# A graph-attention kernel on one core: the next block's preparation spread unevenly over the groups, and further ahead

## The chip, the cores and the metric

The kernel runs on one core of a Trainium2 chip. Its time is device microseconds of one execution. Five engines work side by side, each through its own instructions in the order in which the program issued them: TensorE (PE; matrix products and transposes into PSUM), VectorE (DVE), ScalarE (ACT), GpSimd (POOL; here almost only the issue of gathers by index) and SyncE (SP; the issue of plain transfers). An engine that meets an instruction whose inputs are not there waits, and what stands behind it on that engine waits too.

## The reference

3327 rows (padded to 3328) of 128 features, and a sparse adjacency matrix `adj` with some 64 non-zeros in a row. Layer 0 is an attention with four heads, layer 1 a normalised neighbourhood sum:

```python
    h = jnp.maximum(_layernorm(x, axis=-1), 0.0)
    for each head:
        x1 = h @ w1;  x2 = h @ w2
        E = leaky_relu(x1[:, None, :] + x2[None, :, :], 0.01)
        s = exp(tanh((E @ a) / 8.0) * 8.0) * adj
        s = s / sum(s, axis=-1)
        out = leaky_relu(s @ h @ Wlin.T, 0.01)
    x = x + concatenate(heads) @ w
    # layer 1
    h = jnp.maximum(_layernorm(x, axis=-1), 0.0)
    A = adj + I;  D_inv = A.sum(1) ** -0.5
    x = x + relu((D_inv[:, None] * A * D_inv[None, :]) @ (h @ W.T + b))
```

The scores are wanted only where `adj` is not zero.

## The kernel before

**Blocks, halves, groups.** The rows are cut into 26 blocks of 128. For each row the kernel finds the columns of its non-zeros, gathers those columns' projections from a table in memory (`g`, L597, by GpSimd, 64 gathers a block, plus 4 into `ge`), and works on what it gathered. A block has two halves of 64 rows, a half has nine groups (`NG`, L252). Groups 0 to 7 of a half take two per gathered unit `w`, with 512 pairs of row and column for each head. The ninth group (`m == 8`) takes the overflow buffer `ge`: rows with more neighbours than their slots hold. Counted through a block the groups are 0 to 17; the ninth ones are 8 and 17.

**A group.** `stage_z` (L612) transposes the gathered projections on PE into PSUM `z` (L624), in two parts of two heads with two buffers between them; DVE takes the maximum with the negated projection of the row (L640, 128x1024 values for each part) into `r`. In the ninth group z is made of 8 transposes, four small ones (L627) and four products (L629), DVE's maximum covers only 64 columns a head (L635), and ACT takes the rest with a relu (L637). `stage_r` (L645) then makes the scores with products `s` (L653); it is issued one group behind. After every second group, `finish` (L657) copies the scores (ACT), turns them (PE, L671), adds and weighs them (DVE, L674 to L693, or L709 and L711 for the overflow), and sums with the products `ag` (L702, L721). At the end of a half `close` (L727) finishes the rows.

**The preparation.** `prep(b)` (L353) is a generator that readies block b in at most 72 steps (`NPREP`), each ended by a `yield`. In this order: it makes codes of the non-zeros of a quarter of the columns at a time (DVE, L410), looks through them with eight-wide maxima (L422), and between those turns the block of `adj` (PE, four transposes L365; ACT copy L367; a store to `AT_d`, L370) and multiplies the turned pieces with rows of layer 1 that are already known (`known_step`, PE L379, DVE L385). How many are known grows with the block (`finished`, L345): none up to block 3, up to 22 columns of blocks in the last. Then it takes sums (ACT, L443), asks for the next block of `adj` (L351), selects the lists of columns (DVE, L453 and L456), makes the indices (L463 to L473), handles the overflow (L489 to L546), and projects the block's own rows (PE, `x1b` L553 and `x1n` L559).

**What sets the order.** Nothing reorders the instructions afterwards: the order on each engine is that of the calls. The main loop (L1195) goes over all 468 groups and calls `slot()` six times for each: once before `stage_z`, four times in it, once behind `stage_r`. `slot` (L858) counts places, lets the pending `finish` and `close` generators take a step, and advances the preparation to a step that follows from the count; then it issues gathers for which buffers are free:

```python
        SLOTP = 6 * 2 * NG                       # 108 places a block
        t = state["slot"] / SLOTP
        advance(NPREP * (1 + t + min(1.0, t) * AHEAD))
```

So a block's 72 steps of preparation go evenly over 108 places, two thirds of a step to a place, four steps to a group. With `AHEAD = 0.5`, at the start of block b the preparation of block b+1 stands at its step 36, and that of block b+2 begins with group 9.

Of the kernel before, what the change touches and what calls it, by code (L numbers as in the profile page):

```python
# [231 lines left out]
def _sparse_layers(tc, nc, x, adj, w1, w2, a, wlin, w, gw, gb, gb_sb, gwT, x_sb, dinv, flag, ident, out):  # L232
# [19 lines left out]
    NG = 9  # L252
# [4 lines left out]
    with ExitStack() as l0:  # L257
# [87 lines left out]
        def finished(b):  # L345

            return max(0, 4 * (b // 4) - 2)
# [262 lines left out]


        def stage_z(k, hb, m, slot):  # L612
            n = 4 * P if m < 8 else FOUND * P
            arrived(k, hb, m // 2)
# [30 lines left out]
        def stage_r(k, hb, m, rs):  # L645
            n = 4 * P if m < 8 else FOUND * P + HALF
            at = m % 2
            if state["scores"] is None:
                state["scores"] = ps_s.tile([P, BANK], F32, name="s")
                nc.vector.memset(state["scores"], 0.0)  # L650
            k.s = state["scores"]
            for h in range(H):
                nc.tensor.matmul(k.s[32 * h:32 * h + 2, :n], sel[:, h, 31 - at:33 - at], rs[h // 2][:, h % 2, :n],  # L653
                                 start=(at == 0), stop=(at == 1 or m == 8))
# [151 lines left out]
        NLIST = 42  # L806
        NPREP = 72
        SLOTP = 6 * 2 * NG
        AHEAD = 0.5
        preps = [prep(b, blks[b]) for b in range(NB)]  # L810
        queue = deque()
        done = [0] * NB
        state = {"slot": 0, "fetched": 0, "g": 4, "ge": 1}
        state["early"], state["turn"], state["scores"] = None, -1, None
        ends, tails = [], []

        def advance(upto):

            for b in range(NB):
                while done[b] < NPREP and b * NPREP + done[b] < upto:  # L820
                    if next(preps[b], "end") == "end":
                        done[b] = NPREP
                    else:
                        done[b] += 1
                        assert done[b] < NPREP

        def fetch():
            while state["fetched"] < len(fetches):
                b, hb, w = fetches[state["fetched"]]
                kind = "ge" if b < NB and w == NW else "g"  # L830
                if state[kind] == 0 or (b < NB and not blks[b].ready):
                    return
                state[kind] -= 1
                if b == NB:
                    strip(pieces[w])
                else:
                    gather(b, hb, w)
                    if w == LATE and hb == (b == 0) and b + 1 < NB:
                        queue.append((None, 0, 0, partial(weights, b + 1)))
                state["fetched"] += 1  # L840
# [4 lines left out]
        def issue():  # L845

            queue.popleft()[-1]()

        def trickle():
            while queue:  # L850
                issue()
# [4 lines left out]
                issue()  # L856

        def slot():  # L858
            state["slot"] += 1
            t = state["slot"] / SLOTP  # L860
            for todo in (tails, ends):
                todo[:] = [f for f in todo if next(f, "end") != "end"]
            advance(NPREP * (1 + t + min(1.0, t) * AHEAD))
            fetch()
            trickle()
            if state["early"] is not None and next(state["early"], "end") == "end":
                state["early"] = None
# [6 lines left out]
        early = {s: range(finished(4 * s), finished(4 * s) + BEGUN) for s in (1, 2, 3) if finished(4 * s) + BEGUN < NB - 3}  # L874
# [24 lines left out]
        def begin():  # L899

            work = [(s, j) for s in early for j in early[s]]
            pairs = [work[i:i + PAIR] for i in range(0, len(work), PAIR)]
            if not work:
                return
            thirds = pa.tile([P, NP], F32, name="adjb")[:, :3 * PAIR * BANK].rearrange("p (k j i) -> p k j i", k=3, j=PAIR)

            def bring(k):
                if k < len(pairs):
                    for to, of in columns(thirds[:, k % 3], pairs[k]):
                        nc.sync.dma_start(to, of)  # L910

            for k in range(3):
                bring(k)
            for _ in range(14):
                yield
            po = None
            for i, (s, j) in enumerate(work):
                assert blks[j].closed
                if j == early[s][0]:
                    po = bank()  # L920
                nc.tensor.matmul(po, x_sb[:, j, :], thirds[:, i // PAIR % 3, i % PAIR], start=(j == early[s][0]), stop=(j == early[s][-1]))
                if i % PAIR == PAIR - 1:
                    bring(i // PAIR + 3)
                if j == early[s][-1]:
                    part2 = pv.tile([P, H, P], F32, name="outT").rearrange("p h i -> p (h i)")
                    nc.scalar.copy(part2, po)
                    nc.sync.dma_start(part2_d[:, 4 * s * P:4 * s * P + BANK], part2)
                for _ in range(4):
                    yield
# [44 lines left out]
        def layer1():  # L974
            ending, sums, ins = [], {}, {}
            for i, (s, j) in enumerate(work):
                if i == in_front:
                    yield "all"
                w = min(4, NB - 4 * s) * P
                if s not in sums:  # L980
                    sums[s] = ps_z.tile([P, 2, BANK], F32, name="z")[:, 0]
                if j == min(NB - 1, first_column(s) + 4 * (s not in front)):
                    assert len(ending) < 2
                    ins[s] = strip_in(s)
                nc.tensor.matmul(sums[s][:, :w], x_sb[:, j, :], strips[s, j][:, :w], start=(j == first_column(s)), stop=(j == NB - 1))  # L985
                if i % PIECE == PIECE - 1 or i == len(work) - 1:
                    allow("g")
                ending[:] = [f for f in ending if next(f, "end") != "end"]
                if j == NB - 1:
                    ending.append(strip_out(s, sums.pop(s), *ins.pop(s)))  # L990
                yield "one"
            for e in ending:
                for _ in e:
                    pass

        groups = [(b, hb, m) for b in range(NB) for hb in range(2) for m in range(NG)]
# [192 lines left out]
        with tc.manual_schedule():  # L1189
            fetch()  # L1190
            while queue:
                issue()
            rs = {}
            n = len(groups)
            for i in range(-1, n + 1):  # L1195
                if i + 1 < n:
                    slot()
                if 0 <= i < n:
                    b, hb, m = groups[i]
                    if (b, hb, m) == (max(0, NB - 2), 1, 0):  # L1200
                        state["early"] = begin()
                    rs[i] = stage_z(blks[b], hb, m, slot)
                if 0 <= i - 1 < n:
                    b, hb, m = groups[i - 1]
                    stage_r(blks[b], hb, m, rs.pop(i - 1))
                    if m % 2 or m == NG - 1:
                        ends.append(finish(blks[b], hb, m // 2))
                    slot()
            lay = layer1()
            todo = "one"  # L1210
            while ends or tails or state["early"] is not None:
                slot()
                if todo == "one":
                    todo = next(lay)
            for _ in lay:
                fetch()
                assert not queue
# [60 lines left out]
def kernel(  # L1278
# [26 lines left out]
    gb_sb = const.tile([P, D], F32, name="gb_sb")  # L1305

    _sparse_layers(tc, nc, x, adj, w1, w2, a, wlin, w, gw, gb, gb_sb, gwT, x_sb, dinv, flag, ident, out)


# [46 lines left out]
```

## Time and profile before

| | us |
|---|---|
| median of 3 runs (lowest, highest) | 2523.51 (2521.55, 2527.58) |
| the profiled execution | 2520.29 |
| its span, from the first to the last instruction | 2518.6 |
| its mean granted TensorE clock | 0.982 |
| PE, DVE, ACT, POOL busy | 2283.0, 2091.0, 686.3, 1733.9 |
| first r of group 0 of block 0; of block 25 | 90.7; 2324.5 |

How the page is read. Busy time is the time in which an engine executes; matrix products are pipelined and their ends modelled, so a busy PE is not one at its peak. PEld is PE's loading of weights, which overlaps its products. The costliest groups name line, engine, operation, output<-inputs and the shape, then `xcount | busy us, mean ns | idle time of the engine just before them, and what ended most of it`. The waits name who waited for whom, in total, how often, and the longest. The starts of DVE's maxima (L640, L635) mark the groups in time: the two of each group stand in order, so the first one of every eighteenth group begins a block. Blocks 1 to 24 take 87.4 to 91.6 us each by these starts.

### The profile page before, as it was taken

How to read it: one execution, taken by the hardware profiler on the slowest of the kernel's cores; microseconds unless marked ns; L12 is line 12 of the kernel's file. 1: busy time of each engine (PE TensorE's matmuls, PEld its weight loads, DVE VectorE, ACT ScalarE, POOL GpSimd, SP SyncE). 2: the span in 40 equal slices, each digit the busy share in tenths (PEclk: the TensorE clock that was granted, in tenths of full speed). 3: DMA queues.
4: the chain of work that ended last, by engine and by line, in shares of the span. 5: the costliest groups of instructions: out<-in, count | busy, mean ns of one | idle time of the engine just before them, and what ended most of it. 6: DMA issues, size and time to landing. Idle time of an engine off the chain costs nothing.

```text
span 2518.6 us, 52430 instructions
## 1 busy us (share of the span) xinstructions
PE 2283.0 (91%) x19410; PEld 1577.3 (63%) x19410; DVE 2091.0 (83%) x6478; ACT 686.3 (27%) x1703; POOL 1733.9 (69%) x1822
## 2 busy tenths in 40 slices
PE   6589999989999898999999999999999999999987
PEld 4456666666666666666666666666666666666643
DVE  7688988898898889889889888988988898895623
ACT  4122223223223222322322232232222223222110
POOL 3577777777777776777777777777777777777700
PEclk9799999999999999999999999999999999999999
DMA  9999999999999999999999999999999999999995
GB/s 307 377 359 325 344 340 312 339 358 319 323 356 334 316 341 336 298 333 357 331 317 349 347 311 333 354 321 319 344 339 316 338 348 310 328 325 351 347 275 153
DMA packets 417844, 826.94 MB, mean 328 GB/s; under 512 B 38435, under 2 KB 288815, under 8 KB 414255
## 3 DMA queue, kind: packets, MB, share of 16 engines
q0 software_dynamic: 141440, 619.41, 70.2%
q1 hardware_dynamic: 165343, 147.87, 18.5%
q10 hardware_dynamic: 110800, 56.25, 7.7%
q8 instruction: 156, 2.56, 0.4%
q14 instruction: 105, 0.86, 0.1%
HBM read 754.47 MB, written 113.22 MB: 345 GB/s over the span
## 4 chain that ended last, share of the span: by engine, by line
PE 36%; DVE 27%; DMA 19%; POOL 10%; issue 7%; ACT 1%; SPq 0%; DVEq 0%; ACTq 0%; POOLq 0%
DVE r L640 13%; DMA g<-table,idx 11%; PE z L624 11%; POOL g L597 9%; PE s L653 6%; PE z L629 3%; DVE cand L422 3%; DMA AT_d<-at 3%; PE tr L671 2%; PE ag L702 2%; DVE cand L456 2%; DVE lists L453 2%; DMA g<-AT_d 2%; DVE codes L410 2%; PE z L985 1%
## 5 line engine op out<-in xcount | busy, mean ns | idle before, releaser
L597 POOL DMA_INDIRECT g<-table,idx x1664 | 1611.9, 969 | 606.1 <-issue 416.3
L640 DVE TENSOR_TENSOR r<-z,x1n 128x1024 f32<-128x1024 f32 x832 | 1009.9, 1216 | 33.2 <-PE z L624 31.4
L624 PE MATMUL z<-ident,g 128*128 128x128 f32 x6656 | 918.6, 279 | 127.5 <-DVE r L640 110.6
L624 PEld LDWEIGHTS z<-ident,g 128*128 128x128 f32 x6656 | 746.4, 142 | 334.7 <-DVE r L640 222.2
L653 PE MATMUL s<-r,sel 128*2 128x512 f32 (+1 forms) x3744 | 473.6, 578 | 2.6 <-DVE s L650 1.9
L662 ACT COPY ssb<-s 128x512 f32<-128x512 f32 x260 | 146.9, 565 | 470.9 <-PE s L653 462.5
L422 DVE MAX8 cand<-codes 128x8 f32<-128x52 uint16 x1664 | 215.1, 204 | 0.0
L682 ACT ACTIVATE th<-sc 128x32 f32<-128x32 f32 x260 | 58.2, 224 | 459.8 <-DVE sc L677 422.3
L702 PEld LDWEIGHTS ag<-g,wt 128*32 128x32 f32 x3328 | 98.7, 110 | 120.3 <-issue 105.2
L671 PE MATMUL tr<-ident,ssb 128*128 128x128 f32 x988 | 157.0, 279 | 10.4 <-ACT ssb L662 9.0
L367 ACT COPY at<-tr 128x512 f32<-128x512 f32 (+1 forms) x175 | 97.1, 555 | 225.3 <-PE tr L365 194.1
L629 PE MATMUL z<-oi,x1b 128*128 128x256 f32 x416 | 145.4, 431 | 0.0
L453 DVE MAX8 lists<-cand 128x8 f32<-128x272 f32 (+1 forms) x338 | 133.2, 394 | 2.9
L702 PE MATMUL ag<-g,wt 128*32 128x133 f32 x3328 | 133.5, 278 | 1.5 <-DVE wt L693 1.5
L365 PE MATMUL tr<-ident,adjb 128*128 128x128 f32 x676 | 110.1, 287 | 25.2 <-DMA adjb<-in_adj_dram 17.7
L674 DVE TENSOR_TENSOR sc<-tr,g 128x32 f32<-128x32 f32 x208 | 38.5, 185 | 112.4 <-PE tr L671 112.4
L671 PEld LDWEIGHTS tr<-ident,ssb 128*128 128x128 f32 x988 | 111.0, 141 | 31.2 <-ACT ssb L662 23.4
L597 POOL DMA_INDIRECT ge<-table,idxo x104 | 98.8, 950 | 31.7 <-issue 14.0
L635 DVE TENSOR_TENSOR r<-z,x1n 128x128 f32<-128x128 f32 x104 | 29.9, 289 | 109.2 <-PE z L629 108.7
L637 ACT ACTIVATE r<-z 128x512 f32<-128x512 f32 x104 | 62.0, 597 | 212.5 <-DVE r L635 212.5
L456 DVE MATCH_REPLACE8 cand<-lists,cand 128x272 f32<-128x272 f32 (+1 forms) x312 | 118.1, 379 | 0.0
L410 DVE SCALAR_TENSOR_TENSOR codes<-adjb,code 128x832 uint16<-128x832 f32 x104 | 103.1, 1018 | 13.1 <-DMA adjb<-in_adj_dram 13.1
(201 smaller groups left out, 2446.0 us busy)
## 6 DMA issues: line engine op xcount, KB each, us to landing
adjb<-in_adj_dram SPq DMA_DIRECT2D x26, 1664.0 KB
table<-AT_d SPq DMA_DIRECT2D x26, 1664.0 KB
AT_d<-at ACTq DMA_DIRECT2D x150, 256.0 KB
g<-table,idx POOLq DMA_INDIRECT x1664
table<-img SPq DMA_DIRECT2D x12, 1296.0 KB
adjb<-AT_d SPq DMA_DIRECT2D x72, 128.0 KB
g<-AT_d SPq DMA_DIRECT2D x25, 256.0 KB
g<-AT_d ACTq DMA_DIRECT2D x25, 256.0 KB
```

Of the source, the lines that this page charges most:

```text
L410: nc.vector.scalar_tensor_tensor(codes[:, i], adjb[:, c0:c0 + part], 0.0, code[:, c0:c0 + part], op0=OP.not_equal, op1=OP.mult, accum_out= ...
L422: nc.vector.max(cand[:, c, 8:].rearrange("p (r s) -> p r s", s=32)[:, :, sgm % 32], codes.rearrange("p a b -> p (a b)")[:, sgm % 32 * SEG: ...
L453: nc.vector.max(top, of)
L456: nc.vector.match_replace(out=of, in_to_replace=top, in_values=of, imm_value=0.0)
L597: return nc.gpsimd.indirect_dma_start(out=g[:, t, lo:hi], out_offset=None, in_=tab, in_offset=bass.IndirectOffsetOnAxis(ap=at[:, t:t + 1], ...
L624: nc.tensor.matmul(z[:, i, q * P:(q + 1) * P], g[:, m % 2 * 4 + q, c0:c0 + D], ident, is_transpose=True, start=(q == 0 or m < 8), stop=(m ...
L629: nc.tensor.matmul(z[:, i, :n], k.x1b[:, h * D:(h + 1) * D], k.oi[:, hb * n:(hb + 1) * n], start=False, stop=True, skip_group_check=True)
L640: nc.vector.tensor_tensor(r.rearrange("p h (i s) -> p h i s", s=16), z.rearrange("p h (i s) -> p h i s", s=16), k.x1n[:, 2 * hp:2 * hp + 2 ...
L653: nc.tensor.matmul(k.s[32 * h:32 * h + 2, :n], sel[:, h, 31 - at:33 - at], rs[h // 2][:, h % 2, :n], start=(at == 0), stop=(at == 1 or m = ...
L662: nc.scalar.copy(ssb[:, :nk * P], s[:, :nk * P])
L671: nc.tensor.transpose(pt[:, q, :], ssb[:, q * P:(q + 1) * P], ident)
L702: nc.tensor.matmul(ag[32 * cg:32 * cg + 32, u, :WORK], wt[:, t].rearrange("p h q -> p (h q)"), g[:, t, f0:f0 + WORK], start=(w == 0 and t ...
```

## The change

Each place now counts with a weight. Before the places of a group are called, `state["pace"]` is set: 2.2 in the ninth groups, and (9 - 2.2) / 8 = 0.85 in the eight others of the half, so that a block still counts 108. The share of a block by which preparation runs ahead goes from 0.5 to 0.58, reached in the course of block 0.

```diff
-        AHEAD = 0.5
+        NINTH = 2.2
+        AHEAD = 0.58
...
-        state["early"], state["turn"], state["scores"] = None, -1, None
+        state["early"], state["turn"], state["scores"], state["pace"] = None, -1, None, 1
...
         def slot():
-            state["slot"] += 1
+            state["slot"] += state["pace"]
             t = state["slot"] / SLOTP
...
             for i in range(-1, n + 1):
+                if 0 <= i < n:
+                    state["pace"] = NINTH if groups[i][2] == NG - 1 else (NG - NINTH) / (NG - 1)
                 if i + 1 < n:
                     slot()
                 if 0 <= i < n:
```

In steps of preparation: 8.8 go into a ninth group and 3.4 into each other one, where all had 4. At the start of block b the preparation of block b+1 stands at step 41.8 of 72. Its last three steps and the first six of block b+2's fall into group 8 (the codes of the first half of the columns among them); the transposes and known products of block b+2 begin with group 9 in place of group 10; the last selections and the first list of indices fall into group 17.

## The prediction

> **What bounds the kernel now.** I read the page's busy shares and costliest groups first, then the waits by engine, then the busy time of each engine in stretches of two blocks, and last the program order of both builds against these durations.
>
> The page's busy line (busy us, share of the span, count), its chain shares, and four of its groups (busy, mean ns | idle before, releaser):
>
> ```profile
> PE 2283.0 (91%) x19410; PEld 1577.3 (63%) x19410; DVE 2091.0 (83%) x6478; ACT 686.3 (27%) x1703; POOL 1733.9 (69%) x1822
> PE 36%; DVE 27%; DMA 19%; POOL 10%; issue 7%; ACT 1%; SPq 0%; DVEq 0%; ACTq 0%; POOLq 0%
> L597 POOL DMA_INDIRECT g<-table,idx x1664 | 1611.9, 969 | 606.1 <-issue 416.3
> L640 DVE TENSOR_TENSOR r<-z,x1n 128x1024 f32<-128x1024 f32 x832 | 1009.9, 1216 | 33.2 <-PE z L624 31.4
> L635 DVE TENSOR_TENSOR r<-z,x1n 128x128 f32<-128x128 f32 x104 | 29.9, 289 | 109.2 <-PE z L629 108.7
> L410 DVE SCALAR_TENSOR_TENSOR codes<-adjb,code 128x832 uint16<-128x832 f32 x104 | 103.1, 1018 | 13.1 <-DMA adjb<-in_adj_dram 13.1
> ```
>
> No engine is idle for long: TensorE (PE) 91%, VectorE (DVE) 83%, and GpSimd issues 68 gathers a block at 0.97 + 0.30 us, 86 us of a block's 89. DVE does have one hole: before the ninth group's small maximum L635 it stands for 108.7 us in all.
>
> The waits of PE, DVE and POOL (total us, times, longest):
>
> ```profile
> PE z L624 <- DVE r L640: 112.1, 144, 2.6
> PE tr L379 <- DVE sc L674: 23.7, 22, 2.9
> DVE r L635 <- PE z L629: 108.7, 73, 2.7
> DVE r L640 <- PE z L624: 31.4, 56, 1.3
> POOL g L597 <- PE ag L702: 68.2, 42, 3.6
> PEld tr L379 <- ACT at L367: 13.8, 16, 0.9
> ```
>
> PE and DVE wait for each other in turn, PE for DVE in the ordinary groups, DVE for PE in the ninth. Gathers seldom hold PE up; GpSimd waits for a buffer that PE has not finished with (68.2 us).
>
> Three stretches of block 5 and the same of block 20, cut where DVE starts the first r of a group: groups 0-6, 7-10, 11-17. Columns: stretch and length in us, busy time and count of PE, weight loads, DVE, ACT, POOL, then clock, DMA share, GB/s:
>
> ```profile
> 545.50:578.60 33.10, 30.72 (x291) 22.50 (x290) 30.91 (x85) 7.63 (x26) 25.18 (x27) 1.00 0.97 336
> 578.60:595.70 17.10, 14.89 (x116) 9.50 (x115) 11.01 (x35) 5.16 (x12) 13.14 (x14) 1.00 0.86 270
> 595.70:633.50 37.80, 36.12 (x315) 24.67 (x316) 35.92 (x126) 12.77 (x27) 28.18 (x30) 0.95 1.01 361
> 1880.40:1913.80 33.40, 30.91 (x293) 22.68 (x291) 31.24 (x86) 7.63 (x26) 25.19 (x28) 1.00 0.99 344
> 1913.80:1936.40 22.60, 21.04 (x180) 14.62 (x179) 16.52 (x56) 7.02 (x17) 17.19 (x18) 1.00 0.90 290
> 1936.40:1969.50 33.10, 31.70 (x284) 22.26 (x282) 31.29 (x108) 10.91 (x22) 23.07 (x24) 1.00 1.00 350
> ```
>
> The stretch around the first ninth group (group 8) is PE's: 21.0 of 22.6 us busy in block 20, DVE 16.5. In the others both are at 31 of 33.
>
> **The change, part by part.** No instruction is added or removed: line for line, both builds have the same counts. On GpSimd the order is identical. On SP the only move is that the store of part1 (L387) goes ahead of the load of ge (L589) in late blocks; ge is needed six groups later, so I cost it at 0 (without that cover, one 64 KB store a block). Everything else is where preparation steps fall between the groups. Their DMAs move with them: seven stores L370 on ACT's queue, the loads of hTb and the next adjb on SP's. From the load of adjb to the codes that need it there are still 12 to 13 groups, about 60 us, and in the trace codes waited for it once (13.1 us, at the start): 0. ACT takes the seven copies L367 (0.56 each) and the sum L443 (3.0) with them, at 27% busy: 0, but for the wait in point 4.
>
> I charge each instruction the mean time by which it moves its engine's end on. PE: transposing a piece 0.123 us, sixteen a group; scores L653 8 x 0.118, together 2.91 for an ordinary group; the ninth group 5.25 (8 transposes, 4 x 0.20 for L627, 8 x 0.314 for L629, scores). A preparation's four transposes L365 cost 0.49, its four known products L379 1.14, x1b 0.90, x1n 1.10. DVE: r L640 1.146, codes L410 0.944 with its accumulator read, four MAX8 0.46, a selection 0.5 to 0.8. Summed in program order, us per group 0 to 17 (PE's share of a group is its transposes up to the scores of the group before):
>
> ```
> block 5   PE  before 3.9 4.1 3.4 5.0 4.1 5.1 4.7 5.2 6.5 3.9 4.9 4.4 5.5 3.9 3.9 2.9 3.9 5.3
>           DVE before 4.1 3.4 5.7 4.4 2.9 5.4 5.0 4.4 1.0 5.2 4.8 6.3 5.7 4.5 4.8 4.1 4.3 2.4
>           PE  after  4.7 3.3 3.4 5.0 4.4 4.8 4.7 6.3 5.4 5.5 4.3 3.9 5.5 3.4 3.9 2.9 3.9 5.3
>           DVE after  3.7 4.5 5.2 3.1 3.8 4.8 4.8 4.1 3.8 4.6 5.6 6.0 4.2 4.7 4.0 4.1 3.9 3.4
> block 20  PE  before 3.9 4.1 3.4 5.0 4.1 5.1 4.7 5.2 6.5 3.9 5.4 6.6 6.6 4.5 3.9 2.9 3.9 5.3
>           DVE before 4.1 3.4 5.7 4.4 2.9 5.4 5.0 4.4 1.0 4.7 4.8 6.7 6.4 4.7 4.8 4.1 4.3 2.4
>           PE  after  4.7 3.3 3.4 5.0 4.4 4.8 4.7 6.3 5.4 7.2 6.6 3.9 6.0 3.4 3.9 2.9 3.9 5.3
>           DVE after  3.7 4.5 5.2 3.1 3.8 4.8 4.8 4.1 3.2 4.6 6.0 6.8 4.4 4.7 4.0 4.1 3.9 3.4
> ```
>
> 1. *Codes and four MAX8 into group 8.* DVE's 1.0 there becomes 3.2 to 3.8, in a place where it idled; in the first ninth group this takes nothing from PE. Removed is what the codes cost in group 9: in block 20 PE waited 0.80 us for r L640 and 0.76 for sc L674 there.
> 2. *The transposes and known products follow earlier.* They are PE work, and the known products grow with the block: none up to block 3's, 18 columns in block 22's, which is prepared during block 20. Before, they stood in groups 10 to 13, where DVE is as loaded (6.6 against 6.7). Now they stand in 9 and 10, directly behind x1n and the ninth group: PE 6.3, 5.4, 7.2, 6.6 in a row, 25.5 us where there were 21.1, against DVE's 17.9 (14.9 before). Behind them groups 11 to 17 are left with PE 29.3 and DVE 31.2 (33.7 and 33.3).
> 3. *Preparation in the second ninth group:* selections, DVE 2.4 to 3.4 below PE's 5.3: free.
>
> If each group costs the larger of its two loads, a block changes by -0.5 to -1.5 in blocks 1 to 5, +0.1 in 6 to 9, +0.6 in 10, +1.2 from 11 to 17, +2.0 from 18 to 21, +2.4 in 22 and 23; blocks 1 to 24 sum to **+17.9**. If PE and DVE can lend each other time over a whole stretch (0-6, 7-10, 11-17), blocks 1 to 9 gain 0.9 to 1.7 each, blocks 18 to 21 lose 1.4, and the sum is **-4.3**. How far they lend the trace tells: for block 20 before, the group account gives 91.5, the stretch account 85.5, and its row took 89.1, 0.6 of the way to the group account. So 0.6 x 17.9 - 0.4 x 4.3 = **+9**.
>
> 4. *A new wait.* The known product needs the tile that ACT has just copied (L367). Before, at least 0.49 us of PE work lay between transposes and product, mostly 0.94 to 1.42; now the first pair of each of 22 blocks has none, and 28 more have only 0.49. The trace's row for this wait is 13.8 us in 16 waits, 0.86 each: 22 x 0.86 + 28 x 0.4 = 30; bounds are 0 (DVE is what ends last there) and 50 x 0.86 = 43. Against it goes the wait that this product has now, 23.7 on sc L674. Net **+6**, bounds -24 and +43.
>
> Sum: +15. Against the profiled execution (2518.6 span, 2520.3 in all, 3.2 under the median of the runs) that is 2535.5; on the median, 2523.5 + 15 = **2539**.
>
> [...]
>
> **The rivals.**
> *Faster (about 2500).* The place is group 9: codes no longer stand between PE and r L640. Its price is 0.80 + 0.76 us a block, 24 x 1.56 = 37 us, so 2486 if all of it is kept, 2505 if half is. It decides if PE's lump costs less than that, that is if PE uses its two z buffers to lend over more than two groups. For it: lending over the three stretches already gives a small gain. Against it: late blocks, where the lump has grown by 4.4 us.
> *No change (2523).* GpSimd sets the pace: 68 x 1.25 = 85.0 us a block and about 1.4 of stretched issues; a block before takes 88.9. For it: gaps of 0.30 us nearly throughout. Against: 68.2 us of waits for PE's ag L702.
> *Much slower (2565).* In group 8 the second r L635 now stands behind 2 x 0.944 + 0.46 = 2.35 us of preparation, and ACT's relu and PE's next z behind it. PE has about 5.0 us of other work first (scores, ag, L365, L379, half a z, tr). It shows only if DVE comes to group 8 more than 2.6 us late; today it comes 1.98 us early. Exposed by 1 us in 26 blocks: 2539 + 26 = 2565; fully, 2600.
>
> **How the numbers follow.** The forecast has 0.45 (its own range 2529 to 2552), much slower 0.18, no change 0.13, faster 0.24. A measurement can tell some 0.2%, 5 us. So faster 0.24, same 0.13, slower 0.63. The range takes half of the faster case and the greater part of the much slower one: 2503 to 2570.
>
> **What would show it.** Right: the idle before L635 falls well below 108.7 us; block lengths rise with the block number, from at or below 88.5 early to 90 or more from block 18; groups 7 to 10 of block 20 take 25 to 27 us (22.6 before) and 11 to 17 take 30 to 32 (33.1); PE waits on ACT at L367 appear at L379. Wrong: late blocks as long as early ones; or PE's wait for r L640 falls far below 112 us with groups 7-10 no longer than 24 us, which is the faster case.

## The result, and the profile after

| | us |
|---|---|
| before, median of 4 runs | 2524.17 (2521.55 to 2527.58) |
| after, median of 4 runs | 2591.98 (2587.39 to 2594.64) |
| ratio, with its 95% interval | 1.0266 (1.0246 to 1.0286) |
| span of the profiled execution, before and after | 2518.6 and 2591.7 |

The change costs 67.8 us. The direction was forecast; 2592 lies 22 us above the upper end of the range.

The page of the changed kernel, in the parts shown of before: busy us by engine with its share of the span and the count, then the shares of the chain, then three groups (busy, mean ns | idle before them, releaser):

```profile
PE 2302.9 (89%) x19410; PEld 1590.5 (61%) x19410; DVE 2074.9 (80%) x6478; ACT 677.5 (26%) x1703; POOL 1734.8 (67%) x1822
...
PE 40%; DVE 21%; DMA 15%; POOL 11%; issue 7%; ACT 4%; SPq 1%; DVEq 0%; ACTq 0%; POOLq 0%
...
L597 POOL DMA_INDIRECT g<-table,idx x1664 | 1612.4, 969 | 675.8 <-issue 435.3
L640 DVE TENSOR_TENSOR r<-z,x1n 128x1024 f32<-128x1024 f32 x832 | 1009.2, 1214 | 78.8 <-PE z L624 77.5
...
L410 DVE SCALAR_TENSOR_TENSOR codes<-adjb,code 128x832 uint16<-128x832 f32 x104 | 103.9, 1014 | 13.0 <-DMA adjb<-in_adj_dram 13.0
```

Counts and means of one instruction are those of before, and all four engines have a smaller share of a longer span. On the chain PE rises from 36% to 40% and ACT from 1% to 4%. So the time went into waiting, and into the order of the work.

The waits (total us, times, longest us), first PE's, then DVE's, then GpSimd's:

```profile
PE z L624 <- DVE r L640: 145.2, 133, 2.8
PE tr L379 <- ACT at L367: 25.5, 50, 1.5
PE tr L553 <- DVE agn L792: 23.1, 24, 1.0
PE tr L671 <- ACT ssb L662: 17.7, 26, 2.6
...
DVE sc L674 <- PE tr L671: 156.6, 111, 3.0
DVE r L635 <- PE z L629: 79.6, 30, 2.8
DVE r L640 <- PE z L624: 77.5, 125, 4.5
...
POOL g L597 <- PE ag L702: 143.0, 53, 7.1
```

DVE's wait at the ninth group's L635 fell by 29 us (108.7 before), but its waits at sc L674 and r L640 rose by 43 (from 114.0) and 46 (from 31.4). PE waits 33 us more for r L640, and two waits are new: L379 for ACT's copy, which takes the place of the 23.7 us on sc L674, and L553 for L792. GpSimd's wait doubled.

The same three stretches of blocks 5 and 20 (groups 0-6, 7-10, 11-17; columns as before):

```profile
554.00:587.20 33.20, 29.35 (x276) 20.86 (x275) 30.45 (x87) 7.20 (x25) 24.97 (x28) 1.00 0.96 327
587.20:612.60 25.40, 22.26 (x191) 15.04 (x190) 19.56 (x71) 8.64 (x21) 19.61 (x20) 1.00 0.94 309
612.60:644.80 32.20, 29.73 (x252) 21.19 (x253) 27.16 (x87) 9.26 (x19) 21.26 (x23) 0.95 0.96 341
1937.50:1972.20 34.70, 30.91 (x276) 22.30 (x275) 30.33 (x86) 7.08 (x25) 26.21 (x28) 0.95 0.94 324
1972.20:2000.20 28.00, 26.57 (x223) 18.88 (x223) 20.23 (x74) 8.86 (x21) 17.98 (x18) 1.00 0.86 263
2000.20:2030.70 30.50, 28.11 (x252) 19.79 (x253) 27.32 (x89) 9.25 (x19) 21.72 (x23) 1.00 1.01 358
```

The stretch around the first ninth group took 17.1 and 22.6 us before and takes 25.4 and 28.0; what follows it falls from 37.8 and 33.1 to 32.2 and 30.5. As means over blocks 2 to 23, worked out from the starts of DVE's maxima, the three stretches go from 33.2, 23.1, 32.7 to 33.3, 27.2, 31.6: the lump costs 4.1 us a block, the relief behind it returns 1.1. From 22 blocks that is 67 us. In the records of PE it splits into 52 us more idle time and 15 us more busy time. PE runs at half its clock for 47.8 us of these blocks, where it was 30.7; half of the difference, some 9 us, is an estimate of what the clock has in the 15.

PE's records of block 20 around the ninth group (start, duration, line, tile, shape, count, and in brackets the idle time before and its releaser) show both new waits:

```profile
1968.54 0.49 PE L789 MATMUL tr<-gwT,agn 128*128 128x128 f32 x2
...
1970.04 0.60 PE L671 MATMUL tr<-ident,ssb 128*128 128x128 f32 x4
...
1972.05 1.12 PE L553 MATMUL tr<-w_sb,hTb 128*128 128x512 f32 x2 [0.96 <-DVE agn L792]
...
1981.84 0.65 PE L365 MATMUL tr<-ident,adjb 128*128 128x128 f32 x4
1983.16 1.16 PE L379 MATMUL tr<-at,x_sb 128*128 128x128 f32 x8 [0.68 <-ACT at L367]
...
1986.74 1.16 PE L379 MATMUL tr<-at,x_sb 128*128 128x128 f32 x8 [0.24 <-ACT at L367]
```

L553: the PSUM tile `tr` has two buffers. L789 fills one, L671 the other, and x1b (L553) needs the first again, which DVE still has to read at L792. In the kernel before, L553 came 3.25 us behind L789 and did not wait:

```profile
1910.79 0.49 PE L789 MATMUL tr<-gwT,agn 128*128 128x128 f32 x2
...
1914.04 1.02 PE L553 MATMUL tr<-w_sb,hTb 128*128 128x512 f32 x2
```

Now it is a step earlier: PE is ready for it 2.55 us behind L789 and waits 0.96. L379: transposes L365 end at 1982.5, ACT's copy L367 takes 0.59, and the product directly behind them stands until it is done. PE's next work (L624 at 1984.16) starts only behind it.

### The profile page after: what moved, and what is told of

Same layout as the page of the kernel before. It is cut to its first block, busy times and chain, and to the rows that moved or that the text cites. A ratio compares the mean times of both kernels' runs of the same rounds, so it can differ in the third digit from the quotient of the medians.

```text
span 2591.7 us, 52410 instructions
## 1 busy us (share of the span) xinstructions
PE 2302.9 (89%) x19410; PEld 1590.5 (61%) x19410; DVE 2074.9 (80%) x6478; ACT 677.5 (26%) x1703; POOL 1734.8 (67%) x1822
## 4 chain that ended last, share of the span: by engine, by line
PE 40%; DVE 21%; DMA 15%; POOL 11%; issue 7%; ACT 4%; SPq 1%; DVEq 0%; ACTq 0%; POOLq 0%
PE z L624 11%; DMA g<-table,idx 11%; DVE r L640 10%; POOL g L597 10%; PE s L653 5%; PE ag L721 3%; PE z L629 3%; PE tr L671 3%; PE tr L379 2%; PE tr L365 2%; ACT adjb L443 2%; DVE cand L456 2%; PE z L986 1%; DVE lists L453 1%; DMA table<-img 1%
## 5 line engine op out<-in xcount | busy, mean ns | idle before, releaser
L640 DVE TENSOR_TENSOR r<-z,x1n 128x1024 f32<-128x1024 f32 x832 | 1009.2, 1214 | 78.8 <-PE z L624 77.5
L624 PE MATMUL z<-ident,g 128*128 128x128 f32 x6656 | 921.1, 279 | 151.3 <-DVE r L640 140.4
L624 PEld LDWEIGHTS z<-ident,g 128*128 128x128 f32 x6656 | 756.1, 143 | 318.5 <-DVE r L640 232.0
L422 DVE MAX8 cand<-codes 128x8 f32<-128x52 uint16 x1664 | 220.9, 203 | 0.0
L367 ACT COPY at<-tr 128x512 f32<-128x512 f32 (+1 forms) x175 | 97.4, 557 | 354.6 <-PE tr L365 319.8
L671 PE MATMUL tr<-ident,ssb 128*128 128x128 f32 x988 | 159.5, 283 | 18.0 <-ACT ssb L662 17.7
L702 PEld LDWEIGHTS ag<-g,wt 128*32 128x32 f32 x3328 | 98.7, 110 | 119.3 <-issue 98.9
L674 DVE TENSOR_TENSOR sc<-tr,g 128x32 f32<-128x32 f32 x208 | 38.6, 186 | 155.6 <-PE tr L671 154.0
L671 PEld LDWEIGHTS tr<-ident,ssb 128*128 128x128 f32 x988 | 111.6, 143 | 39.2 <-ACT ssb L662 29.4
L702 PE MATMUL ag<-g,wt 128*32 128x133 f32 x3328 | 133.5, 278 | 1.2 <-DVE wt L693 1.2
L365 PE MATMUL tr<-ident,adjb 128*128 128x128 f32 x676 | 112.9, 290 | 21.3 <-DMA adjb<-in_adj_dram 13.9
L365 PEld LDWEIGHTS tr<-ident,adjb 128*128 128x128 f32 x676 | 79.7, 147 | 64.9 <-issue 22.7
```

Of the source, the lines that this page charges most:

```text
L365: nc.tensor.transpose(pt[:, q, :], adjb[:, (j0 + q) * P:(j0 + q + 1) * P], ident)
L422: nc.vector.max(cand[:, c, 8:].rearrange("p (r s) -> p r s", s=32)[:, :, sgm % 32], codes.rearrange("p a b -> p (a b)")[:, sgm % 32 * SEG: ...
L624: nc.tensor.matmul(z[:, i, q * P:(q + 1) * P], g[:, m % 2 * 4 + q, c0:c0 + D], ident, is_transpose=True, start=(q == 0 or m < 8), stop=(m ...
L640: nc.vector.tensor_tensor(r.rearrange("p h (i s) -> p h i s", s=16), z.rearrange("p h (i s) -> p h i s", s=16), k.x1n[:, 2 * hp:2 * hp + 2 ...
L671: nc.tensor.transpose(pt[:, q, :], ssb[:, q * P:(q + 1) * P], ident)
L702: nc.tensor.matmul(ag[32 * cg:32 * cg + 32, u, :WORK], wt[:, t].rearrange("p h q -> p (h q)"), g[:, t, f0:f0 + WORK], start=(w == 0 and t ...
```

## The experiments

Three theories were tried. *Load* (theory A of the expectations): the products L365, L379 and the projections are too much PE work for groups 7 to 10, and DVE's holes elsewhere don't pay for it. *Codes in group 8* (theory B): the 2.35 us of preparation between the two r L635 of group 8 cost. *Hand-overs*: the work would fit, but pairs of it that hand over between PE, ACT and DVE now stand directly behind one another. The first runs split the change and took away each hand-over alone. Unless said otherwise the edits are to the changed kernel. Each ratio is to the kernel before, run on the same chip; it took 2522.1, 2527.0, 2523.6 and 2524.2 us on the four chips of the runs up to the last heading of this section.

**The shift alone, and the weight in one ninth group alone.**

```diff
-        NINTH = 2.2
+        NINTH = 1.0
```

> The preparation runs 0.58 of a block ahead, but every place counts 1, as before the change. Theory A (where the preparation's PE work falls is what costs: it lands on groups 7 to 10, where PE is the bound; in block 20 the loads there are 4.5, 5.7, 7.2, 6.1 = 23.5 us against 21.1 before and 25.5 changed): most of the 68 us stays, 2545 to 2575 us. Theory B (the weights cost: in the changed kernel codes and four maxima, 2.35 us, stand between the two r L635 of group 8): the loss is gone, 2515 to 2535 us.

```diff
-                    state["pace"] = NINTH if groups[i][2] == NG - 1 else (NG - NINTH) / (NG - 1)
+                    state["pace"] = 1 if groups[i][1] != 0 else NINTH if groups[i][2] == NG - 1 else (NG - NINTH) / (NG - 1)
```

> 0.58 ahead; the weight 2.2 only in the ninth group of the first half (group 8), all places of the second half count 1. Theory A: 2575 to 2600, since groups 7 to 10 are as in the changed kernel (6.3, 5.4, 7.6, 6.1 us of PE in block 20). Theory B: as the changed kernel, 2585 to 2600. If instead the weight in group 17 does the harm (DVE waits 39 us at idx L473 for PE there), 2540 to 2560.

The shift alone gave 2558.6 (ratio 1.0146, 1.0122 to 1.0169), +36.5 us; with 2.2 shares in group 8 it was 2596.4 (1.0290, 1.0269 to 1.0312). So the weight in the first ninth group costs 38 us beyond the shift, and the one in the second gives some 4 back, within the intervals. The two halves lose in different places. PE's waits of the shift alone:

```profile
PE z L624 <- DVE r L640: 171.7, 211, 1.9
PE tr L365 <- DMA adjb<-in_adj_dram: 16.4, 2, 10.6
PE tr L743 <- ACT agn L737: 9.2, 1, 9.2
PE tr L379 <- DVE part L385: 9.1, 6, 1.5
```

It has neither new hand-over, and loses most in groups 0 to 6 (35.1 us a block for 33.2), where DVE is the late one. So 2558.6 lies in theory A's range, but mostly not by its reason, which was the load in groups 7 to 10. With the weight in group 8 the first groups are back at 33.5, and 7 to 10 take 27.1 in place of 24.0; both hand-overs are there now, 18.9 us at L379 for the copy L367 and 22.9 at L553. The time of the second run fits theories A and B alike.

**Each hand-over taken away.** x1b a step later, by moving one empty step ahead of it; and the known product one step behind the copy that it needs:

```diff
             k.ready = True
             yield
 
+            yield
             pm = bank()
...
             yield
-            yield
             pm = bank()
```

> The changed kernel with the product x1b L553 one step of preparation later (one of the two empty steps behind pmx is moved ahead of it). In the changed kernel PE waits there 0.96 us in each of 24 blocks, 23.1 us, for the bank that DVE's agn L792 reads. If that wait is a loss of its own: it goes, and the time falls by 15 to 23 us, to 2569 to 2577. If PE only waits for DVE there in place of elsewhere (rival): the wait turns up before z L624 or at the next product, 2587 to 2595.

```diff
             def known_step(j0, js, at):
                 assert all(blks[j0 + q].closed for q in js)
+                yield
                 pq = bank()
```

> The changed kernel with each known product L379 two to three steps later behind its transposes (an empty step ahead of it): at least 1.5 us of PE work lies between, where there was none in 22 blocks and 0.49 in 28 cases. PE's load in groups 7 to 10 of block 20 goes from 25.5 to 24.3 us, in group 9 from 7.2 to 6.0, in group 11 from 3.9 to 5.0. Theory A: the 25.5 us of waits on ACT's copy L367 go, and PE's idle time in group 11 is filled: 2592 - 25 - 15 = 2552, between 2540 and 2565. Rival (DVE ends last there, or the wait turns up elsewhere): 2585 to 2595.

With x1b later, 2571.3 (1.0198, 1.0175 to 1.0220): 20.6 us back (17 by the ratios), and the wait L553 on L792 is gone from PE's list. With the known product later, 2545.5 (1.0108, 1.0072 to 1.0143): 46.5 us back from an edit that moves nothing on PE but L379. Its PE waits, and PE's records of block 20 where there were the stalls (a line is one number higher):

```profile
PE z L625 <- DVE r L641: 144.3, 138, 2.6
PE tr L554 <- DVE agn L793: 23.2, 24, 1.0
...
PE tr L672 <- ACT ssb L663: 14.4, 28, 1.4
```

```profile
1940.07 1.06 PE L380 MATMUL tr<-at,x_sb 128*128 128x128 f32 x8
1940.97 0.60 PE L365 MATMUL tr<-ident,adjb 128*128 128x128 f32 x4
1941.40 1.04 PE L625 MATMUL z<-ident,g 128*128 128x128 f32 x8
...
1943.02 1.16 PE L380 MATMUL tr<-at,x_sb 128*128 128x128 f32 x8
1944.01 0.60 PE L365 MATMUL tr<-ident,adjb 128*128 128x128 f32 x4
```

The wait on ACT's copy is gone and the one for r L641 has not grown (144.3; 145.2 before the edit): in this stretch PE was what ended last, so all of the wait was time. More came back than the wait's 25.5 us. In the profiled execution PE's time at half clock fell too, from 47.8 to 27.3 us, and its idle time in group 10 from 1.40 to 1.11 us a block. The size is less sure than the direction: the four runs took 2541.5 to 2558.2 us, at granted clocks from 0.980 down to 0.974, and the profiled one is the fastest of them; by the ratios 40 us came back.

**Both together, and the second one in the kernel before.** Both edits to the changed kernel; and the extra `yield` in `known_step` alone, put into the kernel before.

> The changed kernel with x1b one step later and each known product an empty step later, as in e5 and e9, which ran on a chip where the kernel before took 3300 to 3400 us. On a chip where it takes 2520 to 2530: if the two waits are separate losses, the gains add up, 2592 - 20.6 - 46.5 = 2525, between 2518 and 2532. If they are one loss, it is no better than the better of the two, 2540 to 2550.

> The kernel before with the empty step ahead of each known product, as in e6 and e10, on a chip where the kernel before takes 2520 to 2530 us. If the 23.7 us of waits for sc L674 at that product are a loss of their own: 2495 to 2510. If DVE ends last there (rival): the wait turns up at z L624, 2515 to 2527.

The changed kernel with both took 2522.7, ratio 0.9988 (0.9974 to 1.0002): all of the loss is back, and the two gains add within their intervals (20.6 + 46.5 = 67.1). The codes still stand in group 8 there, so theory B falls as well. The kernel before with the product later took 2519.2, ratio 0.9972 (0.9961 to 0.9984). It is the only version here that is measurably faster than the kernel before, by 0.28%. Its waits of PE tell why so little:

```profile
PE z L625 <- DVE r L641: 123.6, 154, 2.6
...
PE tr L365 <- DVE part L386: 8.8, 18, 0.9
PE tr L380 <- DVE sc L675: 7.0, 22, 0.3
```

The 23.7 us on sc L674 became 11.5 more on r L641, 8.8 on part and 7.0 on sc: where the kernel before has this wait DVE ends last, and it is waited for in another place.

**The length of the known products.** In both kernels only the first column of each known product is computed; the rest of that work is left out.

```diff
-                for q in js:
-                    nc.tensor.matmul(pq[:, :P], x_sb[:, j0 + q, :], at[:, q, :], start=(q == 0), stop=(q == js[-1]))
+                for q in js[:1]:
+                    nc.tensor.matmul(pq[:, :P], x_sb[:, j0 + q, :], at[:, q, :], start=True, stop=True)
```

> As e7, on a chip where the kernel before takes 2520 to 2530 us: the changed kernel with only the first column of each known product of up to four (the others are left out, so layer 1 lacks them). L379 goes from 488 to about 136 products, some 50 us of PE work less; order, copies and waits are kept. Theory A (the load in groups 7 to 10 costs beside the waits): these products stand where PE ends last, so the time falls by 35 to 50 us, 2542 to 2557. Rival (the waits alone): 2580 to 2592.

> As e8, on such a chip: the kernel before with one column of each known product (the others are left out). There they stood in groups 10 to 13, where DVE is loaded as much as PE. Theory A expects little, 2505 to 2522; the rival that PE's load counts wherever it stands expects as much as in the changed kernel, 2475 to 2490.

The changed kernel took 2585.3 (1.0252, 1.0229 to 1.0275), 7 us less and within the intervals; the kernel before 2520.7 (0.9995, 0.9984 to 1.0006). The load theory falls, and the rival holds: with the products cut the waits stay whole.

```profile
PE z L624 <- DVE r L640: 149.8, 132, 2.6
PE tr L379 <- ACT at L367: 25.5, 50, 1.5
PE tr L553 <- DVE agn L792: 23.3, 24, 1.0
```

Part of the saving was given back by the clock. In this run PE spends 78.5 us at half clock (47.8 in the changed kernel), all of it in group 11, which is told below. Half of the difference is some 15 us, an estimate; even without it the saving would be 22 us, and theory A asked for 35 to 50.

**The turn later still, and ACT's sum.** To the changed kernel with both edits: the transposes begin at segment 12 in place of 0.

```diff
-                if sgm % 8 == 5 and tab_at < NB:
+                if sgm >= 12 and sgm % 8 == 5 and tab_at < NB:
```

> The kernel of e11 (both waits removed, 2523 us) with the transposes of the preparation beginning one turn later, at the 13th eight-wide maximum and not before: codes stay in group 8, PE's load in groups 7 to 10 of block 20 goes from 24.3 to 22.7 us (6.0 to 4.4 in group 9) and in groups 12 and 13 from 9.4 to 11.1, where DVE has 9.4. Theory A: the larger of the two loads, summed over the groups of blocks 1 to 24, falls by 20 us against e11, so 2500 to 2512, faster than both kernels. Rival (GpSimd's issue sets the pace of 88 to 89 us a block): 2517 to 2525.

It took 2543.6 (1.0073, 1.0045 to 1.0101), 21 us more than without this edit; neither expectation holds. The wait that grew:

```profile
PE z L625 <- DVE r L641: 134.1, 116, 9.8
PE tr L672 <- ACT ssb L663: 41.2, 34, 1.8
```

ACT's sum over `adjb` (2.98 us) comes when the turn ends, and now stood ahead of the copy of the scores that PE's L672 waits for. So the sum, with the load behind it, was moved behind the first selection, in this kernel and in the one without the segment edit:

```diff
-            nc.scalar.activation(adjb, adjb, AF.Copy, accum_out=deg)
-            if 0 < b < NB - 1:
-                load(b + 1)
...
                 yield from select(r)
+                if r == 0:
+                    nc.scalar.activation(adjb, adjb, AF.Copy, accum_out=deg)
+                    if 0 < b < NB - 1:
+                        load(b + 1)
```

> The kernel of e15 (2544 us) with ACT's sum over adj and the load of the next adj behind the first selection instead of ahead of it, so that the copy of the scores stands before the sum. In e15 PE waits 41 us in 34 waits for that copy, 1.8 us each in some 22 blocks. If the sum is the cause: 2544 - 22 x 1.3 = 2515, between 2500 and 2520. If DVE or GpSimd sets that stretch: 2535 to 2545.

> The kernel of e11 (2523 us) with the sum placed in the same way. In e11 PE waits 11.5 us in 33 waits for the copy of the scores. If the sum is the cause: 2511 to 2517, faster than the kernel before; otherwise 2520 to 2526.

The first took 2520.2 (0.9986, 0.9970 to 1.0002), so the place of the sum, with the load behind it, was worth 23.5 us (22 by the ratios), and the wait is down from 41.2 us:

```profile
PE tr L673 <- ACT ssb L664: 6.3, 10, 1.0
```

The second took 2524.9 (1.0002, 0.9985 to 1.0019): no gain, against both expectations, though its wait on the copy of the scores is off the head of PE's list. But for the run with the turn later, every version without the hand-overs ends at 2519 to 2525. GpSimd's issues, with the gaps of 0.3 us between them, take 86 to 87 us of a block's 89 there, but that they are what stops them was not tried.

**Six runs on another chip.** Both edits, the known product later in the kernel before, and the shortened products in both kernels were run first on a chip where the kernel before takes 3322 us, and two of them again when it took 3396.

> The changed kernel with x1b one step later and each known product an empty step later. If the two waits are separate losses, the gains measured one by one add up: 2592 - 20.6 - 46.5 = 2525, between 2518 and 2532, about the time before the change. If they are one loss (whichever is removed, PE arrives at the same bound), it is no better than the better of the two: 2540 to 2550.

> The kernel before with the empty step ahead of each known product. It waits 23.7 us in 22 blocks for sc L674 at that product. If a wait of PE at this place is a loss of its own there too: 2524 - 24 = 2500, between 2495 and 2510. If DVE, late by the codes and the maxima in groups 9 to 11, ends last (rival): the wait turns up at z L624, 2515 to 2527.

> The changed kernel, with only the first column of each known product of up to four computed (the others are left out, so layer 1 lacks them): L379 goes from 488 to about 136 products, some 50 us of PE work less, the order and all copies and waits kept. Theory A (PE's load in groups 7 to 10 is what costs beside the two waits): all of these products stand in groups 9, 10 and 12, so the time falls by 35 to 50 us, 2542 to 2557. Rival (the waits alone): 2580 to 2592.

> The kernel before, likewise with one column of each known product (the others are left out). There the products stood in groups 10 to 13, where DVE is loaded as much as PE (6.7 against 6.6 in group 11 of block 20), so theory A expects little: 2505 to 2522. Rival (PE's load counts wherever it stands): as much as in the changed kernel, 2475 to 2490.

> As e5 (the changed kernel with x1b one step later and each known product an empty step later), on a chip where the kernel before takes 2520 to 2530 us. If the two waits are separate losses, the gains add up: 2592 - 20.6 - 46.5 = 2525, between 2518 and 2532. If they are one loss, it is no better than the better of the two: 2540 to 2550.

> As e6 (the kernel before with the empty step ahead of each known product), on a chip where the kernel before takes 2520 to 2530 us. If the 23.7 us of waits for sc L674 at that product are a loss of their own: 2495 to 2510. If DVE ends last there (rival): the wait turns up at z L624, 2515 to 2527.

| edit | us | ratio to the kernel before there |
|---|---|---|
| both hand-overs taken away | 3344.6 | 1.0062 (1.0029 to 1.0095) |
| the kernel before, known product later | 3288.0 | 0.9893 (0.9857 to 0.9929) |
| changed kernel, products shortened | 3357.9 | 1.0103 (1.0060 to 1.0146) |
| the kernel before, products shortened | 3259.1 | 0.9799 (0.9765 to 0.9832) |
| both hand-overs taken away, again | 3468.2 | 1.0217 (1.0164 to 1.0270) |
| the kernel before, known product later, again | 3374.1 | 0.9930 (0.9907 to 0.9953) |

They settle nothing on the 68 us: on that chip shortening the products gives 2% in the kernel before, where it gives nothing on a chip that takes 2524 us, and "both" is a loss that varies from 0.6% to 2.2%. They are left out of the reasoning, and the later runs above took their place.

## Why the prediction was wrong in size

- *What bounds the kernel.* Right: PE and DVE wait for each other in turn, and groups 7 to 10 are PE's (in block 20 of the changed kernel PE is busy for 26.6 of 28.0 us, DVE for 18.9). PE had room for the lump all the same: without the two hand-overs the kernel stands at 0.9988. Most of the loss is waits, 52 of the 67 us in blocks 2 to 23, and the shares of the span hardly show them: PE went from 91% to 89% and its weight loads from 63% to 61% while the time rose by 2.7%.
- *Points 1 and 3, free places in the ninth groups.* The hole was found, but not filled for profit: L635's wait fell by 29 us, while DVE's idle time in a block rose from 10.5 to 14.2 us. The work in the second ninth group was free, as forecast: DVE waits 39.0 us there for PE's L470 (at L473, in 24 waits), and 38.7 us of that are still there in the kernel with both edits, at 2522.7.
- *Point 2, the lump.* Its place was right: in block 20, groups 7 to 10 were forecast at 25 to 27 us and took 28.0, groups 11 to 17 at 30 to 32 and took 30.5. The growth with the block number was wrong: blocks 2 and 3 take 89.2 us, 4 to 7 91.9, 8 to 11 92.7, 12 to 17 92.5, 18 to 23 92.2 (before: 88.5 to 89.9 throughout). The size of the load was not what set the loss; the shortened products say the same.
- *The sum of point 2, "0.6 x 17.9 - 0.4 x 4.3 = +9".* Without the hand-overs the changed kernel stands at 0.9988, the kernel before with its own known product later at 0.9972: about +4 us between them, and their intervals overlap. The step put too much on load, and not too little.
- *The step that failed, "A new wait ... Net +6".* The wait itself was forecast at 30 us in 50 waits and measured at 25.5 in 50, though the row that gave its price, 13.8 us in 16 waits, was one of PE's weight loads (PEld) and PE's own products had no such row. It was then set off against the 23.7 us on sc L674 as if a microsecond of either were worth the same. Taken away, the new one returned 46.5 us (40 by the ratios) and the old one 7.8 (2527.02 to 2519.24). The old one stood where DVE ended last and went elsewhere when it was removed; the new one stood where PE ended last and was all loss, and in the profiled executions the time at half clock went with it. The net was +39 (33 by the ratios), not +6: inside the bounds that the step gave (-24 to +43), at the end that it did not take.
- *What was not named at all.* L553's wait for a PSUM buffer, 23.1 us in 24 waits, 20.6 us of time by the run without it. No row of before shows it, but the order of both builds does: L553 moved a step closer to L789, and the prediction does not ask who else uses the two buffers of `tr`.
- *Costed at 0: ACT's sum L443.* At most a small error here: PE's wait on the copy of the scores went from 9.0 to 17.7 us, and moving the sum away gained nothing once the hand-overs were gone. The run with the turn later shows that in another place the sum, with the load behind it, can cost 23.5 us.
- *The rivals.* "Much slower" named 2565 to 2600, and the time lies between them, but its cause is not there: in block 20 the z behind the second L635 starts at 1984.16 without a wait. "No change" and "faster" fall. GpSimd is not the pace of the changed kernel: its wait for ag L702 rose from 68.2 to 143.0 us.

The 67.8 us come out as 46.5 for the known product, 20.6 for x1b, and the rest of a few us either way, within the intervals; by the ratios they are 40, 17 and some 10, and the run without both returns all of it. That the shift alone costs 36.5 us is no part of this sum: that kernel has other waits.

## What to carry to other kernels

When steps of a background task are moved in an engine's fixed order, list for every one what it hands to whom and which buffer it takes next, and keep one piece of other work between a producer and its consumer; here one empty step returned 40 to 46 us and another 17 to 21. A wait that goes and a wait that comes may be set off against each other only if the same engine ends last in both places. Look for that in the busy shares of the stretch, not in those of the whole span.

## What the runs showed of the hardware that was not expected

**The clock of TensorE halves in a busy kernel.** Around the start of group 11 of each block PE stands idle, because two pieces of codes and the overflow's small operations stand on DVE together (1.4 us in group 10 and 1.2 in group 11, on average). In 8 of 22 blocks PE's clock is halved there for 3.4 or 6.8 us. Group 11 of blocks 4, 5, 7 and 18 of the changed kernel (length, then busy time and count of PE, weight loads, DVE, ACT, POOL, then the granted clock, DMA share and GB/s):

```profile
520.20:527.80 7.60, 6.37 (x30) 5.89 (x31) 4.23 (x19) 0.59 (x1) 5.77 (x7) 0.62 0.93 299
612.60:619.20 6.60, 5.33 (x31) 4.85 (x31) 4.26 (x19) 0.46 (x1) 5.08 (x6) 0.74 1.00 322
797.90:802.90 5.00, 3.73 (x30) 3.48 (x31) 4.26 (x19) 0.45 (x1) 3.78 (x5) 1.00 0.97 298
...
1815.20:1820.10 4.90, 3.68 (x30) 3.42 (x31) 4.48 (x20) 0.41 (x1) 3.78 (x4) 1.00 0.95 288
```

The same work takes 5.0 us at full clock, 6.6 or 7.6 with a dip: three dips of 1.6 us and five of 2.6, some 18 us. The kernel before had nine short ones in other places. With the products shortened, group 11 has a dip in 14 blocks, among them blocks 18 and 20, where the changed kernel has none:

```profile
1805.20:1812.90 7.70, 6.42 (x30) 5.94 (x31) 4.65 (x21) 0.59 (x1) 5.77 (x7) 0.62 0.96 305
1989.70:1997.50 7.80, 6.57 (x30) 6.10 (x31) 4.68 (x21) 0.59 (x1) 5.92 (x7) 0.60 0.99 317
```

So with less work on PE it ran longer at half clock, in all four runs (granted clocks of 0.964 to 0.970, for 0.976 to 0.978), and a change shifts which blocks are caught. The dip of block 4 in the changed kernel, in the same columns:

```profile
522.02:528.85 6.83, 6.83 (x32) 6.35 (x31) 3.46 (x13) 1.05 (x3) 4.73 (x5) 0.50 0.98 315
```

What sets off a dip was not shown. PE's wait at this place does not by itself: it is as long in block 7, where the clock stays at 1.00. PE's records at the end of this wait in blocks 4 and 7:

```profile
521.43 0.65 PE L624 MATMUL z<-ident,g 128*128 128x128 f32 x4 [2.12 <-DVE r L640]
...
799.17 0.66 PE L624 MATMUL z<-ident,g 128*128 128x128 f32 x4 [2.10 <-DVE r L640]
```

**On one other chip the same program took a third longer.** The kernel before took 3322 and 3396 us there against 2524. In the run with both hand-overs taken away the mean granted clock was 0.893 (0.978 in the same kernel at 2523 us), PE was at half clock for 716 us (116) and busy for 2603.5 (2284.4), and GpSimd waited for ag, while its issues took no longer (0.94 to 0.97 us for 14 of 15 in a stretch of 30 us of the kernel before with the known product later there; 0.97 on average on the faster chip):

```profile
POOL g L598 <- PE ag L703: 839.4, 171, 11.8
```

PE's extra busy time is 319 us; what makes up the rest of the 800 is open.
